# Inverse edge counts of a relational graph layer: narrow one-hots, four array columns, a result kept relation by destination

## The chip, the cores and the metric

The kernel runs on one core of a Trainium2 chip. The core's engines work side by side and meet through semaphores: TensorE (PE) multiplies matrices into PSUM, its weight loads are listed as PEld; VectorE (DVE) and ScalarE (ACT) do elementwise work; GpSimd (POOL) issues the gathers by index; SyncE (SP) issues most other transfers. The metric is the device time of one execution in microseconds, lower is better; times of several executions are given as their median.

## The reference, cut to what matters

A graph of 3125 nodes with 128 features has 103,125 directed edges, sorted by destination, each with a type from 0 to 15. A four-layer graph convolution is followed by three relational layers. One relational layer is:

```python
seg = tgt * R + edge_type                      # R = 16 relations
msg = x[src]
agg = segment_sum(msg, seg, N * R).reshape(N, R, d)
cnt = segment_sum(ones, seg, N * R).reshape(N, R, 1)
agg = agg / clip(cnt, 1.0)
out = einsum('nrd,rdo->no', agg, W_r) + x @ root_r + bias_r
```

The counts depend on the edges alone and are the same in all three layers. So they are made once, and every layer multiplies its sums by 1/max(count, 1).

## The kernel before, in words

The kernel first packs and indexes the edges, then runs the convolution's first three layers (adjacency blocks built from one-hots, multiplied at L811), then the fourth aggregation, then the relational layers. The program is written as interleaved generators and handed to a scheduler that fixes each engine's order when the program is built; at run time every engine works through its list in order.

**The fourth aggregation** (L1195 to L1217, about 1007 to 1158 us of the profile). Seven column groups of up to four node blocks. For each block of 128 nodes, 25 matmuls (L1207, 384 columns) accumulate in a PSUM tile p_a of a four-buffer pool; VectorE evacuates it in three steps (L1212). `first_rows` normalizes finished blocks, transposes them (L1189) and stores them as rows of the table from which the first relational layer gathers.

**The counts** are made in the same time by the generator `relation_tiles`, of which a step is run before most node blocks. The destinations are taken in 49 groups of 64. A group's edges fill at most 18 tiles of 128 edges, so there are 882 tiles, laid out as c (7 sets of groups), k (18 tiles), g (7 groups in a set). A packed word per edge is gathered (L728); `relative` makes the destination within the group, `to_edges` turns it so that edges lie on partitions (transposes at L748, copies at L754). In the same way go the type, the combined key `16 * destination + type`, from which the start of the tile's window is taken off first, and the source index. Since edges are sorted, tile k of a group can only reach the destinations `WIN[k]` of its 64: between 5 and 17 of them.

To count, `hot` (L796) makes two one-hots for 21 tiles at a time: hr, 64 wide, of the destination, and ht, 16 wide, of the type. Each tile is one matmul (L1161): hr as weights (64 columns), ht moving (16 columns), added into PSUM at partitions 0 or 64 by the group's parity. All of it fits one bank, pc: 128 partitions by 400. A maximum with 1 and a reciprocal (L1169 to L1171) give wi, and one transfer writes it to winv_d as rows of destinations with the 16 relations inside (L1172).

**The relational layers** (1165 us to the end) run `rgcn_mixed`. For each of 25 node blocks, `loads` fetches the slots sr and two tiles wv, each 64 destinations' inverse counts broadcast to all partitions (L1346). Even groups are computed from X in place: one-hots G and S (L1421, L1425), matmuls L1445 (four array columns of 32) and L1488 into p_p, a pool of one buffer, with a rest at L1494. Odd groups are computed from gathered messages (L1369): one-hots sel (L1455), matmuls L1469 into p_a, two buffers. Both accumulators hold 32 destinations by 16 relations, relation innermost. `scaled` (L1363) multiplies such an accumulator by its half of wv and writes gs relation by destination, 1024 bytes from one relation to the next. `project` then takes gs relation by relation into the weights (L1379), and `rows_out` stores the new rows. The multiply is done 294 times: 150 from p_p, 144 from p_a. After each p_p multiply the next L1488 starts a new sum in the same buffer.

A second branch, `rgcn_gathered`, holds the same multiply; it is built but not taken with these inputs.

Of the kernel before, what the change touches and what calls it, by code (L numbers as in the profile page):

```python
# [10 lines left out]
F32 = mybir.dt.float32  # L11
F16 = mybir.dt.float16
# [3 lines left out]
ALU = mybir.AluOpType  # L16
# [5 lines left out]
P = 128  # L22
N = 3125
NB = 25
NP = NB * P
NR = 16
# [600 lines left out]
def regular(ctx: ExitStack, tc: tile.TileContext, a: dict, out: bass.AP, c_d, s_d, h_d, dinv):  # L627
# [45 lines left out]
    with ExitStack() as gx:  # L673
# [10 lines left out]
        adj_d = [dram.tile([P, NB * 4 * P], BF, name=f"adj_d{q}") for q in range(NQ)]  # L684
        winv_d = dram.tile([NP, NR], F32, name="winv_d")

# [105 lines left out]

        def hot(pool, numbers, table, width, t0, n, name, room=None):

            o = pool.tile([P, room or n, width], F16, name=name)[:, :n, :]
            nc.vector.tensor_tensor(  # L796
                o.rearrange("p t (c w) -> p t c w", w=2),
                numbers[:, :width].rearrange("p (c w) -> p c w", w=2)[:, None, :, :].to_broadcast([P, n, width // 2, 2]),
                table[:, t0:t0 + n, None, :].to_broadcast([P, n, width // 2, 2]), op=ALU.is_equal)
            return o  # L800
# [321 lines left out]
        def relation_tiles():  # L1122

            with tc.tile_pool(name="tr", bufs=1) as tw, tc.tile_pool(name="trh", bufs=2) as th:
                w, at = gathered_words(tw, RR, TR, 7, CR, GR)
                yield
                rel, d_i = relative(tw, w, at)
                rel2 = tw.tile([P, CR * RR, 2], F16, name="rel2")
                to_edges(tw, rel, RR, CR, dup(rel2, 1))
                typ2 = tw.tile([P, CR * RR, 2], F16, name="typ2")  # L1130
                typ = tw.tile([RR, CR, P], F32, name="typ")
                nc.vector.tensor_scalar(d_i, w, 12, NR - 1, op0=ALU.logical_shift_right, op1=ALU.bitwise_and)
                nc.vector.tensor_copy(typ, d_i)
                to_edges(tw, typ, RR, CR, dup(typ2, 0))
                yield
                nc.vector.scalar_tensor_tensor(rel, rel, float(NR), typ, op0=ALU.mult, op1=ALU.add)
                lo_f = tw.tile([RR, 1], F32, name="lo_f")
                nc.vector.memset(lo_f, 0.0)
                p_f = tw.tile([RR, 1], F32, name="pr_f")
                iota(nc, p_f, [[0, 1]], 1)  # L1140
                more = tw.tile([RR, 1], F32, name="more")
                for k in range(1, TR):
                    nc.vector.tensor_scalar(more, p_f, 7.0 * k, float(NR * (WIN[k][0] - WIN[k - 1][0])),
                                            op0=ALU.is_ge, op1=ALU.mult)
                    nc.vector.tensor_add(lo_f, lo_f, more)
                nc.vector.tensor_scalar(rel, rel, lo_f, None, op0=ALU.subtract)
                to_edges(tw, rel, RR, CR, dup(key2, 1))
                nc.vector.tensor_scalar(d_i, w, 4095, None, op0=ALU.bitwise_and)
                nc.vector.tensor_copy(typ, d_i)
                to_edges(tw, typ, RR, CR, lambda t0, m, p: nc.vector.tensor_copy(src_t[:, t0:t0 + m], p))  # L1150
                yield
                pc = ps_b.tile([P, 512], F32, name="p_b")
                for c in range(CR):
                    for k0 in range(0, TR, 3):
                        t0 = c * RR + k0 * 7
                        hr = hot(th, iota_k, rel2, GR, t0, 21, "hr")
                        ht = hot(th, iota_k, typ2, NR, t0, 21, "ht")
                        for t in range(21):
                            g = c * 7 + t % 7
                            o = 64 * (g % 2)  # L1160
                            nc.tensor.matmul(pc[o:o + 64, (g // 2) * NR:(g // 2 + 1) * NR], hr[:, t, :], ht[:, t, :],  # L1161
                                             start=(c == 0 and k0 == 0 and t < 2),
                                             stop=(c == CR - 1 and k0 == TR - 3 and t >= 19), skip_group_check=True)
                    yield
                wi = tw.tile([P, NB, NR], F32, name="wi")
                nc.vector.memset(wi, 1.0)
                full = (NB - 1) * NR
                wf = wi.rearrange("p b r -> p (b r)")
                nc.vector.tensor_scalar_max(wf[:, :full], pc[:, :full], 1.0)  # L1169
                nc.vector.tensor_scalar_max(wf[:64, full:], pc[:64, full:NB * NR], 1.0)  # L1170
                nc.vector.reciprocal(wf, wf)  # L1171
                nc.sync.dma_start(winv_d.rearrange("(b p) r -> p b r", p=P), wi)  # L1172
                yield
# [50 lines left out]
    def rgcn_gathered(xT):  # L1224
        with ExitStack() as rx:
# [44 lines left out]
            for l in range(3):  # L1270
# [7 lines left out]
                for b0 in range(0, NB, 2):  # L1278
# [3 lines left out]
                    for g in groups:  # L1282
                        wv = wvp.tile([P, GR * NR], F32, name="wv")
                        nc.sync.dma_start(wv, winv_d[g * GR:(g + 1) * GR, :].rearrange("n r -> (n r)")[None, :]
                                          .to_broadcast([P, GR * NR]))
                        for h, p in enumerate(gathered(g, tabs[l % 2])):
                            n0 = (g - 2 * b0) * GR + 32 * h
                            nc.vector.tensor_tensor(gs[:, :, n0:n0 + 32].rearrange("p r n -> p n r"),
                                                    p.rearrange("p (n r) -> p n r", r=NR),
                                                    wv[:, h * 512:(h + 1) * 512].rearrange("p (n r) -> p n r", r=NR),  # L1290
                                                    op=ALU.mult)
# [24 lines left out]
    def rgcn_mixed(X):  # L1316

        with ExitStack() as rx:
# [20 lines left out]
            def loads(b):  # L1339
# [4 lines left out]
                for g in range(2 * b, min(2 * b + 2, NGR)):  # L1344
                    t = wvp.tile([P, GR * NR], F32, name="wv")
                    nc.sync.dma_start(t, winv_d[g * GR:(g + 1) * GR, :].rearrange("n r -> (n r)")[None, :]  # L1346
                                      .to_broadcast([P, GR * NR]))
                    wv.append(t)
                return sr, wv

            def layer(l, X, Xn):
# [9 lines left out]

                def scaled(gs, p, wv, n0):
                    nc.vector.tensor_tensor(gs[:, :, n0:n0 + 32].rearrange("p r n -> p n r"),  # L1363
                                            p.rearrange("p (n r) -> p n r", r=NR),
                                            wv.rearrange("p (n r) -> p n r", r=NR), op=ALU.mult)

# [41 lines left out]
                for at, b in enumerate(order):  # L1408
# [10 lines left out]
                    for q in range(4):  # L1419
# [18 lines left out]
                        for half in range(2):  # L1438
# [12 lines left out]
                            for _ in range(plan[2 * q + half] if two else 0):  # L1451
# [23 lines left out]
                                if k == TR:  # L1475
                                    for h in range(2):
                                        scaled(gs, pa[h], wv[1][:, h * 512:(h + 1) * 512], b % 2 * P + GR + 32 * h)
                            if todo:
# [4 lines left out]
                            def spread(pb=pb, m=m, S=S, q=q, half=half, b=b, gs=gs, wv=wv, Sx=Sx if q % 2 else None,  # L1483
# [8 lines left out]
                                if q % 2 and half:  # L1492
                                    for i in range(3):
                                        nc.tensor.matmul(pb, mx[:, i, :], Sx, start=False, stop=(i == 2),  # L1494
                                                         skip_group_check=True)
                                    scaled(gs, pb, wv[0][:, q // 2 * 512:(q // 2 + 1) * 512], b % 2 * P + 32 * (q // 2))
                                    if q == 3 and (b % 2 or b == NB - 1):
# [43 lines left out]
```

## Time and profile before

| | us |
|---|---|
| median of 3 runs | 3061.7 (3061.36 to 3063.99) |
| profiled execution, its time | 3064.4 |
| its span in the profile | 3062.5 |
| PE / DVE / POOL / ACT busy | 2700.7 / 1800.2 / 1456.5 / 1088.2 |
| one-hots hr and ht (L796) | 42 x 850 ns and 42 x 319 ns |
| count matmuls (L1161) | 882 |
| maxima and reciprocal (L1169, L1170, L1171) | 0.56, 0.16 and 2.63 |
| multiply by inverse counts (L1363) | 294 x 1044 ns |

The span is that of one execution under the profiler, so sums are made against it and then carried to the median. A busy share says how long an engine worked, not whether anything waited for it; the chain of work that ended last follows, step by step back from the end, what released what. A matmul's end is modelled, so its start-to-start distance is the better measure of its cost.

### The profile page before, as it was taken

What the parts mean: (1) busy time and instruction counts of PE and PEld (TensorE: products, weight loads), DVE (VectorE), ACT (ScalarE), POOL (GpSimd) and SP (SyncE); (2) the same over time, 40 slices, a digit from 0 to 9 for tenths busy, and PEclk for the clock granted to TensorE, in tenths of its full rate; (3) what the DMA queues carried; (4) which work ended last, traced back from release to release, by engine and by line L of the source; (5) the groups of instructions that cost most, each with busy time, mean ns of one, the idle gap of its engine ahead of it and who ended that gap; (6) DMA issues with size and microseconds to landing.
All of it is one profiled execution on the core that took longest, in us unless ns stands there. A gap on an engine that the chain in (4) does not pass through costs nothing.

```text
span 3062.5 us, 62721 instructions
## 1 busy us (share of the span) xinstructions
PE 2700.7 (88%) x25427; PEld 1797.7 (59%) x25427; DVE 1800.2 (59%) x3710; ACT 1088.2 (36%) x2657; POOL 1456.5 (48%) x1472
## 2 busy tenths in 40 slices
PE   0377679999999897999999999999999999999998
PEld 0244345545555564777666666666666666667666
DVE  6886886757663784555555445454555455545453
ACT  0333433222222213444444344343444443434343
POOL 4100000000000005777777757777777577777775
PEclk9988879999999997999999999999999999999999
DMA  5111113222211535555555545555555455555553
GB/s 162 33 70 60 44 44 141 87 88 99 88 60 44 191 129 156 163 153 153 162 151 149 153 138 157 147 155 146 162 145 152 124 155 151 151 149 151 150 151 90
DMA packets 179105, 386.78 MB, mean 126 GB/s; under 512 B 49831, under 2 KB 128902, under 8 KB 175732
## 3 DMA queue, kind: packets, MB, share of 16 engines
q1 hardware_dynamic: 100708, 232.22, 23.3%
q0 software_dynamic: 68480, 141.38, 16.8%
q10 hardware_dynamic: 9616, 9.08, 1.0%
q8 instruction: 201, 3.29, 0.4%
q14 instruction: 100, 0.82, 0.1%
HBM read 350.25 MB, written 32.30 MB: 125 GB/s over the span
## 4 chain that ended last, share of the span: by engine, by line
PE 69%; DVE 15%; DMA 11%; issue 3%; POOL 1%; ACT 1%; another core or an unknown queue 0%; DVEq 0%; POOLq 0%; SPq 0%; ACTq 0%
PE p_p L1488 18%; PE p_a L811 15%; DMA msg<-tab,src_t 9%; PE p_m L1379 9%; PE p_g L1445 8%; PE p_a L1469 8%; DVE gs L1363 3%; PE p_a L1207 3%; DVE ov L796 2%; DVE ou L796 2%; PE p_m L825 2%; PE p_b L874 2%; PE p_p L1494 1%; DMA seg<-f_d,at_i 1%; POOL msg L1369 1%
## 5 line engine op out<-in xcount | busy, mean ns | idle before, releaser
L1369 POOL DMA_INDIRECT msg<-tab,src_t x1296 | 1325.6, 1023 | 400.1 <-issue 110.6
L1447 ACT CAST m<-p_g 128x384 bf16<-128x384 f32 x1800 | 748.9, 487 | 738.8 <-PE p_g L1445 737.6
L1488 PE MATMUL p_p<-S,m 128*128 128x256 bf16 x5400 | 697.6, 274 | 21.0 <-DVE gs L1363 16.0
L1425 DVE TENSOR_TENSOR S<-iota_k,key_s 128x1536 bf16<-128x1536 f16 x300 | 287.5, 959 | 629.2 <-PE p_p L1488 628.8
L1488 PEld LDWEIGHTS <-m 128*128 128x128 bf16 x5400 | 488.8, 98 | 260.3 <-issue 206.6
L1469 PE MATMUL p_a<-sel,msg 128*128 128x144 bf16 (+9 forms) x4536 | 437.9, 239 | 91.0 <-DMA msg<-tab,src_t 89.9
L1469 PEld LDWEIGHTS <-msg 128*128 128x128 bf16 x4536 | 342.5, 98 | 165.8 <-DMA msg<-tab,src_t 100.1
L1455 DVE TENSOR_TENSOR sel<-iota_k,key 128x1248 bf16<-128x1248 f16 (+2 forms) x216 | 198.7, 920 | 133.1 <-PE p_a L1469 133.0
L1445 PE MATMUL p_g<-X,G 128*32 128x384 bf16 x4800 | 273.2, 331 | 0.2
L1379 PE MATMUL p_m<-gs,Wr 128*128 128x256 f32 (+1 forms) x1248 | 267.1, 372 | 1.7 <-DVE gs L1363 1.7
L874 PE MATMUL p_b<-ov,ou 128*128 128x200 f16 x1200 | 169.9, 293 | 111.0 <-DVE ou L796 88.9
L1379 PEld LDWEIGHTS p_m<-gs,Wr 128*128 128x128 f32 x1248 | 230.5, 191 | 32.9 <-DVE gs L1363 2.8
L1445 PEld LDWEIGHTS <-G 128*32 128x32 bf16 x7200 | 138.0, 95 | 143.3 <-issue 88.7
L874 PEld LDWEIGHTS <-ou 128*128 128x128 f16 x1200 | 119.9, 113 | 161.0 <-DVE ou L796 125.9
L811 PE MATMUL p_a<-adj,x3b 128*128 128x512 bf16 (+1 forms) x1050 | 212.8, 356 | 0.0
L1421 DVE TENSOR_TENSOR G<-sr,pid 128x768 bf16<-128x768 f16 x300 | 166.4, 555 | 77.1 <-PE p_g L1445 70.9
L811 PE MATMUL p_a<-adj,x3a 128*128 128x512 bf16 (+1 forms) x1050 | 211.1, 356 | 0.0
L413 POOL IOTA pp<- 128x1 f32 x1 | 0.1, 138 | 414.6 <-PE p_b L874 414.6
L1363 DVE TENSOR_TENSOR gs<-p_a,wv 128x512 f32<-128x512 f32 x144 | 150.4, 1044 | 38.6 <-PE p_a L1469 34.2
L1363 DVE TENSOR_TENSOR gs<-p_p,wv 128x512 f32<-128x512 f32 x150 | 156.6, 1044 | 8.2 <-PE p_p L1494 8.2
L811 PEld LDWEIGHTS <-x3a 128*128 128x128 bf16 x1050 | 95.3, 98 | 97.4
L811 PEld LDWEIGHTS <-x3b 128*128 128x128 bf16 x1050 | 95.7, 98 | 95.4
(343 smaller groups left out, 2505.1 us busy)
## 6 DMA issues: line engine op xcount, KB each, us to landing
wv<-winv_d SPq DMA_DIRECT2D x147, 512.0 KB
adj<-adj_d SPq DMA_DIRECT2D x18, 3200.0 KB
sr<-slots_d SPq DMA_DIRECT2D x75, 768.0 KB
msg<-tab,src_t POOLq DMA_INDIRECT x1296
adj_d<-adj SPq DMA_DIRECT2D x6, 3200.0 KB
tab<-X SPq DMA_DIRECT2D x50, 96.0 KB
adj<-adj_d SPq DMA_DIRECT2D x3, 800.0 KB
tab<-Xn SPq DMA_DIRECT2D x25, 96.0 KB
```

The lines of the kernel that those rows point to most:

```text
L811: nc.tensor.matmul(p[k][:, :n], x3_[:, i, s, k * P:(k + 1) * P], adj[:, i, :n], start=(i == 0 and s == 0), stop=(i == NB - 1 and s == 2))
L874: nc.tensor.matmul(pb[:, gg * IA:(gg + 1) * IA], hot_u[k][:, g + gg, :], hot_v[k][:, g + gg, :], start=(gg == 0 and k == 0), stop=(gg == 1 ...
L1363: nc.vector.tensor_tensor(gs[:, :, n0:n0 + 32].rearrange("p r n -> p n r"), p.rearrange("p (n r) -> p n r", r=NR), wv.rearrange("p (n r) - ...
L1369: nc.gpsimd.indirect_dma_start(out=m.rearrange("p s d -> p (s d)"), out_offset=None, in_=table, in_offset=bass.IndirectOffsetOnAxis(ap=at, ...
L1379: nc.tensor.matmul(po[:, :n], W[:, r, :], gs[:, r, :n], start=False, stop=(r == NR - 1))
L1421: nc.vector.tensor_tensor(G.rearrange("p (c w) -> p c w", w=2), sr[:, q, :].rearrange("p (c w) -> p c w", w=2), pid[:, None, :].to_broadca ...
L1425: nc.vector.tensor_tensor(S.rearrange("p j (c w) -> p j c w", w=2), iota_k[:, :GS * NR].rearrange("p (c w) -> p c w", w=2)[:, None, :, :] ...
L1445: nc.tensor.matmul(pg[o:o + 32, :3 * D], G[:, i * 32:(i + 1) * 32], X[:, i, :, :].rearrange("p s d -> p (s d)"), start=True, stop=True)
L1447: nc.scalar.copy(m[:, t, :], pg[:, :3 * D])
L1455: nc.vector.tensor_tensor(s6[:, :, :n6].rearrange("p j (c w) -> p j c w", w=2), iota_k[:, :n6].rearrange("p (c w) -> p c w", w=2)[:, None, ...
L1469: nc.tensor.matmul(pa[h][:, (a0 - 32 * h) * NR:(a1 - 32 * h) * NR], msgs[k][:, i, :], s6[:, k % 6, (a0 - lo) * NR:(a1 - lo) * NR], start=( ...
L1488: nc.tensor.matmul(pb[:, o:o + GS * NR], m[:, t, i * D:(i + 1) * D], S[:, 3 * half + t, :], start=(q % 2 == 0 and half == 0 and t == 0 and ...
```

## The change

The counts are made the other way round, narrower, and kept the other way round:

- The window's start is taken off the destination before it is turned (and the result is cut at 100), so rel2 holds numbers within the window, 0 to 16. The key is made from rel2 and typ2 where the edges already lie on partitions; its own turning, seven transposes and two copies, goes.
- One-hots are made for 42 tiles (six k) at a time. hr is only as wide as the widest window among them: 14, 16 or 18 in rows of 18. ht stays 16 wide.
- The matmul has ht as weights (16 columns) and hr's window moving (6 to 18 columns). Its result is 16 relations on partitions, destinations along the row. Group g goes to partitions 32 * (g % 4), columns of bank g // 32: two banks, four array columns. `ends` marks the first and last matmul of each bank and column.
- Maxima and reciprocal are done in two batches, after set 4 and after the last set, over 16 of every 32 partitions. wi is set to 1 by POOL.
- winv_d is kept as group, relation, destination, written by four transfers, one for each array column.
- The multiply reads wv by relation inside destination, at a distance of 64 words from one relation to the next.

```diff
-        winv_d = dram.tile([NP, NR], F32, name="winv_d")
+        winv_d = dram.tile([NGR, NR, GR], F32, name="winv_d")
...
-        def hot(pool, numbers, table, width, t0, n, name, room=None):
-
-            o = pool.tile([P, room or n, width], F16, name=name)[:, :n, :]
+        def hot(pool, numbers, table, width, t0, n, name, room=None, wide=None):
+
+            o = pool.tile([P, room or n, wide or width], F16, name=name)[:, :n, :width]
...
                 rel, d_i = relative(tw, w, at)
+                lo_f = tw.tile([RR, 1], F32, name="lo_f")
+                nc.vector.memset(lo_f, 0.0)
+                p_f = tw.tile([RR, 1], F32, name="pr_f")
+                iota(nc, p_f, [[0, 1]], 1)
+                more = tw.tile([RR, 1], F32, name="more")
+                for k in range(1, TR):
+                    nc.vector.tensor_scalar(more, p_f, 7.0 * k, float(WIN[k][0] - WIN[k - 1][0]),
+                                            op0=ALU.is_ge, op1=ALU.mult)
+                    nc.vector.tensor_add(lo_f, lo_f, more)
+                nc.vector.tensor_scalar(rel, rel, lo_f, 100.0, op0=ALU.subtract, op1=ALU.min)
...
-                nc.vector.scalar_tensor_tensor(rel, rel, float(NR), typ, op0=ALU.mult, op1=ALU.add)
-                lo_f = tw.tile([RR, 1], F32, name="lo_f")
...
-                nc.vector.tensor_scalar(rel, rel, lo_f, None, op0=ALU.subtract)
-                to_edges(tw, rel, RR, CR, dup(key2, 1))
+                nc.vector.scalar_tensor_tensor(key2, rel2, float(NR), typ2, op0=ALU.mult, op1=ALU.add)
...
-                pc = ps_b.tile([P, 512], F32, name="p_b")
+                pc = [ps_b.tile([P, 512], F32, name="p_b") for _ in range(2)]
+                wi = tw.tile([P, 13, GR], F32, name="wi")
+                nc.gpsimd.memset(wi, 1.0)
+                wf = wi.rearrange("p g n -> p (g n)")
+                seen = {}
                 for c in range(CR):
-                    for k0 in range(0, TR, 3):
+                    for k in range(TR):
+                        for g in range(7 * c, 7 * c + 7):
+                            seen.setdefault((g // 32, g % 4), []).append((c, k, g))
+                ends = {v[i]: i for v in seen.values() for i in (0, -1)}
+                for c in range(CR):
+                    for k0 in range(0, TR, 6):
                         t0 = c * RR + k0 * 7
-                        hr = hot(th, iota_k, rel2, GR, t0, 21, "hr")
-                        ht = hot(th, iota_k, typ2, NR, t0, 21, "ht")
-                        for t in range(21):
-                            g = c * 7 + t % 7
-                            o = 64 * (g % 2)
-                            nc.tensor.matmul(pc[o:o + 64, (g // 2) * NR:(g // 2 + 1) * NR], hr[:, t, :], ht[:, t, :],
-                                             start=(c == 0 and k0 == 0 and t < 2),
-                                             stop=(c == CR - 1 and k0 == TR - 3 and t >= 19), skip_group_check=True)
+                        wd = (max(WIN[k][1] - WIN[k][0] for k in range(k0, k0 + 6)) + 2) // 2 * 2
+                        hr = hot(th, iota_k, rel2, wd, t0, 42, "hr", wide=18)
+                        ht = hot(th, iota_k, typ2, NR, t0, 42, "ht")
+                        for t in range(42):
+                            k, g = k0 + t // 7, c * 7 + t % 7
+                            lo, hi = WIN[k]
+                            o, n0 = 32 * (g % 4), g // 4 % 8 * GR
+                            nc.tensor.matmul(pc[g // 32][o:o + NR, n0 + lo:n0 + hi + 1], ht[:, t, :],
+                                             hr[:, t, :hi + 1 - lo], start=ends.get((c, k, g)) == 0,
+                                             stop=ends.get((c, k, g)) == -1, skip_group_check=True)
+                    if c in (4, CR - 1):
+                        h, c0, c1 = (0, 0, 512) if c == 4 else (1, 512, 13 * GR)
+                        for i in range(4):
+                            m = c1 - c0 if h == 0 or i == 0 else c1 - c0 - GR
+                            nc.vector.tensor_scalar_max(wf[32 * i:32 * i + NR, c0:c0 + m],
+                                                        pc[h][32 * i:32 * i + NR, :m], 1.0)
+                        nc.vector.reciprocal(wf[:, c0:c1], wf[:, c0:c1])
                     yield
-                wi = tw.tile([P, NB, NR], F32, name="wi")
-                nc.vector.memset(wi, 1.0)
-                full = (NB - 1) * NR
-                wf = wi.rearrange("p b r -> p (b r)")
-                nc.vector.tensor_scalar_max(wf[:, :full], pc[:, :full], 1.0)
-                nc.vector.tensor_scalar_max(wf[:64, full:], pc[:64, full:NB * NR], 1.0)
-                nc.vector.reciprocal(wf, wf)
-                nc.sync.dma_start(winv_d.rearrange("(b p) r -> p b r", p=P), wi)
+                for i in range(4):
+                    n = len(range(i, NGR, 4))
+                    nc.sync.dma_start(winv_d[i:NGR:4, :, :].rearrange("g r n -> r g n"), wi[32 * i:32 * i + NR, :n, :])
...
-                    nc.sync.dma_start(t, winv_d[g * GR:(g + 1) * GR, :].rearrange("n r -> (n r)")[None, :]
+                    nc.sync.dma_start(t, winv_d[g].rearrange("r n -> (r n)")[None, :]
...
-                def scaled(gs, p, wv, n0):
+                def scaled(gs, p, wv, n1, n0):
                     nc.vector.tensor_tensor(gs[:, :, n0:n0 + 32].rearrange("p r n -> p n r"),
                                             p.rearrange("p (n r) -> p n r", r=NR),
-                                            wv.rearrange("p (n r) -> p n r", r=NR), op=ALU.mult)
+                                            wv.rearrange("p (r n) -> p n r", r=NR)[:, n1:n1 + 32, :], op=ALU.mult)
```

## The prediction

> **What bounds the kernel now.** I read the page's totals first, then the chain of work that ended last, then two stretches closely: the fourth aggregation, where the counts are made, and the relational stage, where they are used. The table of stretches (us from the span's start; after each engine's time the instructions that touch the stretch):
>
> ```profile
> core 0: us, PE busy (x) PEld busy (x) DVE busy (x) ACT busy (x) POOL busy (x), PEclk, DMA share, GB/s
> ...
> 1056.90:1121.20 64.30, 64.17 (x1131) 39.89 (x1131) 60.87 (x173) 6.64 (x26) 0.00 (x0) 1.00 0.38 143
> 1121.20:1165.00 43.80, 37.21 (x226) 21.78 (x224) 30.73 (x116) 11.29 (x44) 0.13 (x1) 0.98 0.32 91
> ...
> 1210.00:3062.00 1852.00, 1744.18 (x18727) 1245.98 (x18726) 956.28 (x1364) 769.00 (x1909) 1370.08 (x1339) 0.99 0.52 148
> ```
>
> The counts fill the first of these; TensorE has no gap there and VectorE is 95% busy. The third is the relational stage, 1852 of 3062.5 us, with TensorE at 94% and VectorE at 52%. Inside the count stretch TensorE's timeline alternates:
>
> ```profile
> 1062.99 0.55 PE L1161 MATMUL p_b<-ht,hr 128*64 128x16 f16 x21
> 1063.47 0.82 PE L1207 MATMUL p_a<-x3a,adj 128*128 128x384 bf16 x4
> 1064.22 0.55 PE L1161 MATMUL p_b<-ht,hr 128*64 128x16 f16 x21
> ```
>
> A period is 1.23 us: four aggregation matmuls, and 21 count matmuls from 1062.99 to 1063.47. Aggregation matmuls alone follow each other every 0.1625 us (60 in 9.75 us at 1130), so four are 0.65. The block of counts costs 0.58: the first block of 42 ran at 20.4 ns each, so 21 are 0.43, and 0.15 goes on changing over and back.
>
> In the relational stage VectorE multiplies each finished accumulator by the inverse counts (L1363). Groups by shape, then the chain in order of time at one such place, then the waits:
>
> ```profile
> L1363 DVE TENSOR_TENSOR gs<-p_p,wv 128x512 f32<-128x512 f32 x150 | 156.6, 1044 | 8.2 <-PE p_p L1494 8.2
> L1363 DVE TENSOR_TENSOR gs<-p_a,wv 128x512 f32<-128x512 f32 x144 | 150.4, 1044 | 38.6 <-PE p_a L1469 34.2 <-PE p_m L1379 4.0
> ...
> L1057 DVE TENSOR_TENSOR F<-t,fe 128x125 f16<-128x125 f16 x4 | 2.7, 677 | 0.0
> ...
> L1042 DVE TENSOR_TENSOR fe<-fe,tm 128x125 f32<-128x125 f32 x4 | 1.2, 290 | 0.1
> ```
> ```profile
> 1504.10 0.19 issue
> 1504.29 1.06 DVE gs L1363
> 1505.35 0.04 issue
> 1505.39 1.14 PE p_p L1488 x9
> ```
> ```profile
> PE p_p L1488 <- DVE gs L1363: 16.0, 64, 0.4
> ```
>
> The waits make L1363 look harmless: 16 us. The chain does not. The pool behind p_p holds one buffer, so the next group's first L1488 matmul cannot start until the multiply has read it. Over the trace's records, 117 of 149 such multiplies have an L1488 matmul starting 52 to 53 ns after their end. TensorE happened to be busy until shortly before, so the wait looks short; there is no slack. From 1210 to the end the chain gives L1363 5.6%, that is 104 us or 99 multiplies. So each nanosecond on L1363 costs 99 to 117 ns of time; I take 105 times. The p_a multiplies have slack, because that pool has two buffers and nothing restarts on their end.
>
> [...]L1363 writes gs in steps of 256 words. L738 fixes the base, 896 elements in 1092 ns and 1664 in 1889, so 1.04 ns each plus 162. Then (1044-162)/512 = 1.72 ns. L1057, with 2-byte data and both a source and the result strided by small steps, costs 3.1 ns per element over L1042 of the same width.[...]
>
> **The change, part by part.**
>
> *The multiply reads across.* wv now holds 16 rows of 64, and L1363 walks it by relation inside destination: each element hops 64 words where it came in runs of 16. Destination and PSUM operand stay. No row of this trace shows a source hop beside a destination hop. Lower bound: it hides under the write hop, 0. Upper bound: the same penalty again, (1.72-1.04)x512 = 348 ns[...].[...] I take 110[...]. 105 x 0.110 = **+11.6 us**[...]. The order of instructions in the relational stage is the same on every engine, and wv's loads carry the same bytes, still 4 KB in a run.
>
> *Count matmuls.* 882 before and after, now with 16 columns of weights and 6 to 18 moving columns in four column groups. In the built program they stand in 15 stretches between other TensorE work, where the trace has 41: 26 x 0.152 = **-4.0 us**. [...]I take 18, 882 x 2.4 ns = **-2.1 us**, bounds 0 and -9.
>
> *One-hots.* Before, 42 x 850 + 42 x 319 ns = 49 us of VectorE. By the slope between the 336- and 1536-wide rows (0.533 ns each plus 140), widths 588, 672 and 756 cost 453, 498 and 543, seven of each, and 21 of 672 cost 498: 21 us. The 28 us are worth nothing by themselves: TensorE had no gap to close. They pay for what follows.
>
> *Inverse counts.* Before 3.7 us (memset, two maxima, reciprocal at 2.63). After: maxima 4 x 0.69 + 0.49 + 3 x 0.43, reciprocals by 6.6 ns a column 3.4 + 2.1: 10 us of VectorE. The first batch stands between two count blocks: 2.8 + 0.5 + 3.4 us before the next one-hot. TensorE has some 6.5 us of other work queued there. With pairs of blocks that meet a just-finished one-hot, **+1.5 us** (0 to 3). The memset goes to POOL, idle from 1007.4 until the word gather at 1019.7; a late one would cost its microsecond. The inverse counts leave in four transfers of 256-byte runs, not one: three more SP issues at 0.38 us near 1125, ahead of the last rows' stores, and first read after 1165. Nothing, with 40 us of cover.
>
> *Front.* The subtraction of window starts (0.68 us) now precedes the first transposes, on which TensorE waits 5.70 us. Its 34 small operations stay in the gather's shadow at 1009 to 1019. The third set of transposes is that of the sources, and the keys come from one VectorE operation on 1764 elements: [...]ahead of the evacuations that TensorE waits for at 1042.69. Queued behind it also stand two one-hots more. Together the restart is 0.4 to 2.5 us later; from it goes the 1.1 us of source transposes later on, and two casts (2.1 us of VectorE, hidden). **+1.3 us**, net.
>
> Sum: 11.6 - 4.0 - 2.1 + 1.5 + 1.3 = +8.3 us. On the profiled execution, span 3062.5 and time 3064.4, that is 3070.8 and 3072.7; on the median of the runs, 2.7 us lower, **3070**.
>
> **The rivals.**
> - *A, partial adding (0.52).* As summed: [...]7 to 15 us against 3 saved; 3064 to 3077.
> - *B, the read hop hides (0.23).* If the source's penalty overlaps the write's, the relational stage is unchanged and the count stage decides: -3, or -10 if the count matmuls fall to 10 ns, +3 if evacuations and keys hold TensorE up. 3052 to 3065, centre 3058. The point is a multiply below 1044 + 30 ns. For it: [...]a stretch where TensorE is full.[...]
> - *C, the penalties add (0.25).* The multiply takes 1.39 us or more, 105 x 0.35 = +37, less 3: 3096[...]. For it: L1057 shows 3 ns extra with strides on both sides. Against: those steps are small, of 2-byte data.
>
> **How the numbers follow.** 0.2% is 6 us, about what can be told from no change. B gives a third of its chance to faster (0.09), the rest to same (0.14); A's low end, a quarter of it, adds 0.13 to same; the rest of A and all of C are slower: 0.64. The range leaves out B's low end and C's upper half: 3056 to 3100.[...]
>
> **What would show it.** L1377, the multiply's new line, at 1.10 to 1.19 us, its chain share from 1210 on rising from 5.6% to above 6%, and that stage longer by about 105 times the difference. A multiply at 1.05 means B, above 1.35 C. Count matmuls (L1173) at 18 ns and 15 stretches; the aggregation's last matmul 3 us earlier than 1158. The prediction falls if the multiplies with 53 ns to the next L1488 gain slack, or if L1173 runs slower than 20.4 ns.

## The result, and the profile after

| | before | after |
|---|---|---|
| median of 4 runs each, us | 3062.84 (3061.36 to 3065.45) | 3095.34 (3092.64 to 3097.15) |
| ratio, 95% interval | | 1.0104 [1.0087, 1.0122] |
| span of the profiled execution | 3062.5 | 3093.9 |
| first gather of the relational stage starts at | 1166.1 | 1161.6 |
| from there to the end | 1896.5 | 1932.2 |

The change makes the kernel 1% slower. The front and the counts gain 4.4 us; the relational stage, whose instructions stand in the same order on every engine, loses 35.8. The table of stretches after (us from the start; then each engine's busy time) answers to the one of before:

```profile
core 0: us, PE busy (x) PEld busy (x) DVE busy (x) ACT busy (x) POOL busy (x), PEclk, DMA share, GB/s
...
1056.90:1121.20 64.30, 58.61 (x1179) 35.51 (x1179) 54.74 (x179) 9.98 (x40) 0.13 (x1) 1.00 0.42 159
1121.20:1165.00 43.80, 32.74 (x198) 19.19 (x195) 25.62 (x89) 8.84 (x35) 2.75 (x3) 0.90 0.37 101
1210.00:3093.00 1883.00, 1752.27 (x18663) 1244.32 (x18661) 985.84 (x1362) 767.26 (x1905) 1401.96 (x1335) 0.99 0.51 145
```

In the count stretch TensorE was busy for 64.17 of 64.30 us; it now has 5.7 us of gaps. In the relational stage (last line, 31 us longer than its counterpart) TensorE gained 8 us of busy time, VectorE 30 and POOL 32. The front and the counts on TensorE's timeline:

```profile
1035.54 1.71 PE L748 MATMUL p_b<-ident,rel 126*128 126x126 f32 x7 [7.50 <-DVE rel L1138]
...
1045.04 9.12 PE L1221 MATMUL p_a<-x3a,adj 128*128 128x384 bf16 x40 [2.35 <-DVE x_sb L1226]
...
1060.68 0.82 PE L1173 MATMUL p_b<-hr,ht 128*16 128x6 f16 x84
```

From the first of 84 count matmuls to the aggregation matmul after them it takes 0.76 us, 9.0 ns each; counted in this way, the first 42 of the old form took 20.4 each. From start to start inside a block without gaps it is 7.0 to 7.8 ns, where it was 18.1 to 18.5. In the trace the moving side has 5 to 17 columns, not 6 to 18. The first line waits 7.50 us, 1.8 more than before, and the aggregation restarts at 1045.04, 2.35 later.

The multiply, and the gathers, from the page's groups after (then mean ns of one, then idle time just before it):

```profile
L1383 POOL DMA_INDIRECT msg<-tab,src_t x1296 | 1357.2, 1047 | 398.6 <-PE p_a L1483 113.2
...
L1377 DVE TENSOR_TENSOR gs<-p_a,wv 128x512 f32<-128x512 f32 x144 | 158.1, 1098 | 38.5 <-PE p_a L1483 34.0
L1377 DVE TENSOR_TENSOR gs<-p_p,wv 128x512 f32<-128x512 f32 x150 | 163.5, 1090 | 9.4 <-PE p_p L1508 9.4
```

and the gathers' group before, which the prediction did not show:

```profile
L1369 POOL DMA_INDIRECT msg<-tab,src_t x1296 | 1325.6, 1023 | 400.1 <-issue 110.6 <-PE p_a L1469 110.0 <-PE p_p L1488 65.5
```

The multiply takes only 50 ns more. The gathers, which the change does not touch, take 24 ns more each, 31.6 us in all, about what the kernel lost (32.5). The idle time before them is the same, 400.1 and 398.6 us, or 0.31 us each, whatever it is put down to. The waits and the chain after, at a place like the one shown of before:

```profile
PE p_a L1483 <- DMA msg<-tab,src_t: 107.1, 86, 13.8
...
PE p_p L1502 <- DVE gs L1377: 19.6, 69, 0.4
```
```profile
1337.63 0.19 issue
1337.82 1.11 DVE gs L1377
1338.94 0.04 issue
1338.98 1.14 PE p_p L1502 x9
```

TensorE's wait for gathered messages was 89.9 us in 69 waits; it is now 107.1 in 86. The chain still runs through the multiply, and 114 of 149 (117 before) still have an L1502 matmul 53 ns after their end. But the multiply's share of the chain fell from 5.6% to 5.2%, where the prediction wanted it above 6%.

### The profile page after: what moved, and what is told of

The parts are those of the page before. It is cut to its first block, busy times and chain, and to the rows that moved or that the text cites. A ratio compares the mean times of both kernels' runs of the same rounds, so it can differ in the third digit from the quotient of the medians.

```text
span 3093.9 us, 62653 instructions
## 1 busy us (share of the span) xinstructions
PE 2699.3 (87%) x25420; PEld 1789.7 (58%) x25420; DVE 1815.0 (59%) x3672; ACT 1087.7 (35%) x2657; POOL 1492.0 (48%) x1473
## 4 chain that ended last, share of the span: by engine, by line
PE 66%; DVE 16%; DMA 12%; issue 3%; ACT 1%; POOL 1%; another core or an unknown queue 0%; DVEq 0%; POOLq 0%; ACTq 0%; SPq 0%
PE p_p L1502 18%; PE p_a L811 15%; DMA msg<-tab,src_t 10%; PE p_g L1459 9%; PE p_m L1393 8%; PE p_a L1483 8%; DVE gs L1377 3%; DVE ov L796 2%; DVE ou L796 2%; PE p_a L1221 2%; PE p_m L825 2%; PE p_b L874 2%; PE p_p L1508 1%; DMA seg<-f_d,at_i 1%; DVE S L1439 1%
## 5 line engine op out<-in xcount | busy, mean ns | idle before, releaser
L1383 POOL DMA_INDIRECT msg<-tab,src_t x1296 | 1357.2, 1047 | 398.6 <-PE p_a L1483 113.2
L1502 PE MATMUL p_p<-S,m 128*128 128x256 bf16 x5400 | 700.3, 275 | 25.8 <-DVE gs L1377 19.6
L1502 PEld LDWEIGHTS <-m 128*128 128x128 bf16 x5400 | 489.6, 98 | 266.5 <-issue 209.8
L1483 PE MATMUL p_a<-sel,msg 128*128 128x144 bf16 (+9 forms) x4536 | 443.4, 240 | 108.5 <-DMA msg<-tab,src_t 107.1
L1377 DVE TENSOR_TENSOR gs<-p_a,wv 128x512 f32<-128x512 f32 x144 | 158.1, 1098 | 38.5 <-PE p_a L1483 34.0
L1377 DVE TENSOR_TENSOR gs<-p_p,wv 128x512 f32<-128x512 f32 x150 | 163.5, 1090 | 9.4 <-PE p_p L1508 9.4
L946 POOL DMA_INDIRECT w<-c_d,at x4 | 4.8, 1206 | 306.2 <-DMA slots_d<-ro 294.7
```

The source lines that it names most:

```text
L1383: nc.gpsimd.indirect_dma_start(out=m.rearrange("p s d -> p (s d)"), out_offset=None, in_=table, in_offset=bass.IndirectOffsetOnAxis(ap=at, ...
L1483: nc.tensor.matmul(pa[h][:, (a0 - 32 * h) * NR:(a1 - 32 * h) * NR], msgs[k][:, i, :], s6[:, k % 6, (a0 - lo) * NR:(a1 - lo) * NR], start=( ...
L1502: nc.tensor.matmul(pb[:, o:o + GS * NR], m[:, t, i * D:(i + 1) * D], S[:, 3 * half + t, :], start=(q % 2 == 0 and half == 0 and t == 0 and ...
```

## What the gathers say

GpSimd issues 1371 gathers from 1161.6 on. Summed over the trace of each kernel (us), the relational stage from the first gather to the end is:

| | before | after |
|---|---|---|
| the gathers' own durations | 1404.3 | 1439.0 |
| gaps under 0.4 us between gathers, some 304 ns each | 416.2 (1366 gaps) | 416.5 (1367) |
| longer gaps (the two between layers hold 46 and 49) | 52.8 (4) | 53.0 (3) |
| after the last gather | 23.2 | 23.7 |
| the stage | 1896.5 | 1932.2 |

GpSimd is never idle for longer than some 0.30 us between gathers except at four places. Its queue of gathers is full from end to end, and it bounds the stage, though the page shows it busy for 74% and TensorE for 94%. So what lengthens gathers lengthens the kernel, microsecond for microsecond: +34.7 and +35.8.

And what lengthens them? A gather during which VectorE does nothing, or only multiplies, takes 942 to 963 ns in both traces (median 946 to 947). Of the 392 gathers over 980 ns of before (after 1200 us), 391 started while a one-hot (S, Sx, G or sel) ran on VectorE and end 808 to 830 ns after that one-hot's end. After the change 465 of 466 started under a one-hot; 433 end 813 to 828 ns after its end, and 32 as long after the end of the next one, which followed at once.

Who starts first decides. The gathers that started before a one-hot, by as little as 10 ns, were never lengthened: 446 before and 371 after, all of 941 to 963 ns. Of those that started under a one-hot with over 160 ns left of it, 391 of 397 were lengthened before and 463 of 468 after, and the 11 others had started within 33 ns of it. Of those that started under the multiply in the same way (147 before, 136 after), none was lengthened, so the hop in the multiply does not slow a gather directly.

The one-hots compare two operands in SBUF; the multiply, under which none of 147 and 136 gathers was lengthened, reads one from SBUF and one from PSUM. In these two traces the two kinds differ in that, among other things. The number of operands in SBUF does not settle it: run a_gts below has a one-hot that reads one tensor from SBUF and still holds gathers (71 of 94). By what means a one-hot holds a gather, no run shows; measured is the end, some 820 ns after the one-hot's, where an undisturbed gather takes 945 in all.

The same place in both traces, VectorE and then POOL, each time first before and then after:

```profile
1339.76 1.05 DVE L1363 TENSOR_TENSOR gs<-p_a,wv 128x512 f32<-128x512 f32 x1
1340.65 0.54 DVE L1421 TENSOR_TENSOR G<-sr,pid 128x768 bf16<-128x768 f16 x1
1341.11 0.99 DVE L1455 TENSOR_TENSOR sel<-iota_k,key 128x1632 bf16<-128x1632 f16 x1
```
```profile
1339.30 1.37 POOL L1369 DMA_INDIRECT msg<-tab,src_t  x1 [0.30 <-PE p_a L1469]
1340.97 1.04 POOL L1369 DMA_INDIRECT msg<-tab,src_t  x1 [0.30 <-issue]
1342.31 0.95 POOL L1369 DMA_INDIRECT msg<-tab,src_t  x1 [0.30 <-issue]
```
```profile
1334.15 1.11 DVE L1377 TENSOR_TENSOR gs<-p_a,wv 128x512 f32<-128x512 f32 x1
1335.18 0.54 DVE L1435 TENSOR_TENSOR G<-sr,pid 128x768 bf16<-128x768 f16 x1
1335.65 0.99 DVE L1469 TENSOR_TENSOR sel<-iota_k,key 128x1632 bf16<-128x1632 f16 x1
```
```profile
1333.72 1.33 POOL L1383 DMA_INDIRECT msg<-tab,src_t  x1 [0.30 <-PE p_a L1483]
1335.36 2.10 POOL L1383 DMA_INDIRECT msg<-tab,src_t  x1 [0.30 <-issue]
1337.77 0.96 POOL L1383 DMA_INDIRECT msg<-tab,src_t  x1 [0.30 <-PE p_a L1483]
```

The second gather of each is the same one. Before, it started 0.32 us after G and ended at 1342.01, 0.82 after G's end. After, G starts 1.03 us after the multiply in place of 0.89, the gather meets it 0.18 us after its start, and ends at 1337.46, 0.82 after the end of sel: it lost G and then all of sel. Gathers over 1.9 us: none before, 23 after. Over all gathers after 1200 us, the time above 945 ns is 105.9 us before and 140.6 after; the part tied to the end of sel grew from 12.9 to 39.5, that of Sx from 0.1 to 6.7, that of G from 25.4 to 28.9, and that of S fell from 66.2 to 64.2.

Note the 0.89 and 1.03. Where another instruction follows at once, the multiply's start to the next start went from 896 to 997 ns for p_p and from 891 to 1006 for p_a (medians): 101 and 115 ns more, or some 1.95 ns per word. Its result comes only 50 ns later, because the overlap with the next instruction shrank from 155 to 98 ns. The mean duration hides half of what the change costs VectorE.

## The experiments

Chips of two kinds served. On the first kind, as in the comparison above, before takes about 3064 us; on the second it takes about 3634, nearly all of the difference in the relational stage, so each ratio below is against before on the same chip. The first four runs fell on a chip of the second kind. The theories then: T1, the multiply's length is amplified in the loop of multiply, TensorE and gathers; R1, the hopping access itself disturbs; R2, the new layout and earlier start do it. The expectations of the first runs call T1 theory 1 and R2 theory 2.

**b_hop: the hop alone, in the kernel before.**

```diff
-                                            wv.rearrange("p (n r) -> p n r", r=NR), op=ALU.mult)
+                                            wv.rearrange("p (r n) -> p n r", r=NR)[:, n1:n1 + 32, :], op=ALU.mult)
```

> The kernel before, with the multiply reading the inverse counts across (64 words from one element to the next, so they are the wrong counts); nothing else differs, also no engine's order. Theory 1, the hop lengthens the multiply by some 50 ns and the relational stage makes more of it than 105 times that: multiply 1.09 us, time 3098 (+35, of which 5 direct). Theory 2, the hop adds only its 50 ns on the path and the rest of the loss lies in the new layout or in the earlier start of the relational stage: 3068.

Measured: 3645.20 us, ratio 1.0043 [1.0028, 1.0058], some +15.5 us by the ratio, with the multiply at 1080 and 1092 ns.

**a_runs: the change without the hop** (the reverse of that edit, in the changed kernel).

> The changed kernel, with the multiply reading the inverse counts in runs of 16 as before (so the wrong ones); count stage and layout stay new. Theory 1: the relational stage is back to its old length, and the count stage's gain of about 6 us is all that is left: 3057. Theory 2: only the direct 5 us go: 3090.

Measured: 3625.38 us, 0.9984 [0.9971, 0.9997], multiply 1035 and 1041 ns. With b_hop this puts a loss on the multiply's read and leaves the count stage a small gain. The change itself was not run on this chip, so R2 stood until b_hop_2.

**b_split: the multiply in two halves, in the kernel before.**

```diff
-                    nc.vector.tensor_tensor(gs[:, :, n0:n0 + 32].rearrange("p r n -> p n r"),
+                    for h in range(2):
+                        o = 256 * h
+                        nc.vector.tensor_tensor(gs[:, :, n0 + 16 * h:n0 + 16 * h + 16].rearrange("p r n -> p n r"),
...
```

> The kernel before, the multiply cut in two of 256 elements each, reading in runs; result unchanged. No hop, but each pair takes longer by one fixed cost[...]. If any lengthening is multiplied (theory 1 in its plain form), 3062 plus five times 294 x 0.1, so +60 to +120. If the loss belongs to the hop[...], only the direct cost shows: 105 x 0.1, +8 to +17, 3070 to 3079.

Measured: 3625.81 us, 0.9984 [0.9964, 1.0003]. It looks like the fall of T1 and is not, since the two halves together take no longer than the whole: see b_split_2.

**a_rel: the even groups' accumulator also relation by destination.** The keys of the even groups are renumbered, so that their multiply reads and writes adjacent words in all operands.

```diff
-                        nc.vector.scalar_tensor_tensor(fr[:, 4, :], rel, float(NR), t, op0=ALU.mult, op1=ALU.add)
+                        nc.vector.scalar_tensor_tensor(fr[:, 4, :], t, float(GS), rel, op0=ALU.mult, op1=ALU.add)
...
+                def scaled_rel(gs, p, wv, n1, n0):
+                    nc.vector.tensor_tensor(gs[:, :, n0:n0 + 32].rearrange("p r (q n) -> p q r n", q=2),
+                                            p.rearrange("p (q r n) -> p q r n", q=2, r=NR),
...
```

> The changed kernel with the keys of S and Sx ordered type x 16 + destination, so that p_p also is relation by destination and its multiply runs over 16 adjacent words in all three operands; the p_a multiply still hops. p_p's multiply 0.70 us instead of 1.09. Theory 1 and the prediction's step that p_p's multiply is on the path: at least 105 x 0.39 = 41 us less than the changed kernel, 3054, and down to 3030 if more is made of it. If the p_p multiplies have slack, under 10 us less: 3087.

Measured: 3621.86 us, 0.9968 [0.9954, 0.9982], the even groups' multiply at 685 ns.

The second four fell on a chip of the first kind.

**after_2: the change again.**

> The changed kernel once more, beside the kernel before on the chip that this batch gets. On the chip of the first comparison it took 32 us more than before; on the chip of the first four experiments before itself takes 570 us more, and the parts of the change tried there add up to about +8 us (hop +15.5, count stage -8). If the extra time of the change is a property of the program (every theory so far), this run shows +32 us on a chip where before takes about 3063 us, and about +8 us (ratio 1.002) on one where it takes about 3634 us.

Measured: 3094.41 us, 1.0087 [1.0067, 1.0106].

**b_hop_2.**

> The kernel before with nothing changed but the order in which the multiply reads its inverse counts (hopping 64 words; the values it meets are then those of other destinations, so its numbers are not the reference's). On a chip where before takes about 3063 us: T1 and R1, by which the multiply's form alone does the harm in the relational stage, give +30 to +40 us; R2, by which the new layout of the count stage and the earlier start of the gathers do it, gives +6 us (115 path multiples of 50 ns) or less. On one where before takes about 3634 us: +15 us again.

Measured: 3105.34 us, 1.0122 [1.0103, 1.0142], +41 us between the medians and +37 by the ratio. The hop alone does all of the harm, and R2 falls: the stage lasts 1941.3 us here and 1941.1 in after_2, whose first gather starts 5.1 us earlier thanks to its count stage. The groups of this run show the changed kernel's gathers, without its counts:

```profile
L1369 POOL DMA_INDIRECT msg<-tab,src_t x1296 | 1371.6, 1058 | 398.7 <-PE p_a L1469 112.0 <-issue 100.8 <-PE p_g L1445 66.7
```

**b_split_2.**

> The kernel before with each multiply cut in two halves, same values, each pair some 150 ns longer than the whole. T1, by which it is the length of the multiply that is amplified in the loop of multiply, TensorE and gathers (36 us for 50 ns): +60 to +120 us on a chip where before takes about 3063 us. R1, by which the hop and not the length does the harm: 115 path multiples of 150 ns, +17 us, or less where the first half's result is early. On one where before takes about 3634 us: within 10 us of before.

Measured: 3063.65 us, 0.9997 [0.9988, 1.0007]. Its groups:

```profile
L1371 POOL DMA_INDIRECT msg<-tab,src_t x1296 | 1328.9, 1025 | 396.7 <-issue 112.1 <-PE p_a L1471 106.7 <-PE p_p L1490 62.8
...
L1365 DVE TENSOR_TENSOR gs<-p_p,wv 128x256 f32<-128x256 f32 x300 | 156.4, 602 | 8.9 <-PE p_p L1496 8.9
```

Two halves of 602 ns are not 1204: the second starts 440 ns after the first, and the pair lasts 1043 on average, as the whole did (1044). Nothing was made longer, so nothing was tested; the gathers (1025 ns) and the time stayed.

**a_rel_2.**

> The changed kernel with the keys of the even groups renumbered (destination*16+type becomes type*16+destination within a tile of 16), so that their multiply goes over adjacent words in all three operands: 685 ns in place of 1090 on the other chip, the odd groups' multiply stays at 1090. If the even groups' multiply is what sets the relational stage's time: 115 path multiples of -400 ns off the changed kernel's +32, about -14 us against before on a chip where before takes about 3063 us. If the odd groups' hop is what disturbs, the time stays above before, at +10 to +30 us.

Measured: 3041.75 us, 0.9922 [0.9903, 0.9942]: faster than both kernels, by 22.6 us than before and 53 than the change. Its groups:

```profile
L1389 POOL DMA_INDIRECT msg<-tab,src_t x1296 | 1303.2, 1006 | 398.7 <-issue 113.1 <-PE p_a L1489 101.3 <-PE p_p L1508 68.2
...
L1382 DVE TENSOR_TENSOR gs<-p_p,wv 128x512 f32<-128x512 f32 x150 | 102.5, 683 | 8.6 <-PE p_p L1514 8.6
```

Only 3 of 150 even multiplies now have a matmul bound to their end, so TensorE's path through the multiply is gone. By time alone the path theory comes near here, with -14 us expected of it and -22.6 measured; what tells it apart is that the stage again follows the gathers: their sum is 1381.3 us, 23.0 less than before, and the stage 1874.6, 21.9 less.

The next three fell on a chip of the second kind again. They were to part the even groups' multiply from the odd ones', and length from access.

**b_hop_pp and b_hop_pa: the hop in one kind of multiply** (in the kernel before, `scaled` kept for the other).

> The kernel before with the hopping read in the even groups' multiply (p_p) alone; its inverse counts are then those of other destinations. Hopping in both multiplies cost 41 us. The path theory (the even groups' multiply is what TensorE waits for, the odd groups' has slack): all of it, +30 to +45 us. If the odd groups' multiply matters as much (it delays the release of message buffers and the next one-hots on VectorE): about half, +15 to +25 us.

> The kernel before with the hopping read in the odd groups' multiply (p_a) alone. The path theory, and the step of the prediction that gave these multiplies slack: within 5 us of before. If what counts is VectorE's time as a whole, which shifts the one-hots against the gathers: +15 to +25 us.

Measured: 3642.97 us, 1.0021 [1.0008, 1.0034], for the even groups; 3641.58, 1.0024 [1.0010, 1.0038], for the odd ones. By the ratios that is +7.6 and +8.7 us, each about half of b_hop's +15.5: on this kind of chip the odd groups' multiplies have no slack either.

**b_long: longer without a hop.**

```diff
+                    nc.vector.tensor_tensor(gs[:, :, n0 + 30:n0 + 32].rearrange("p r n -> p n r"),
+                                            p[:, 480:].rearrange("p (n r) -> p n r", r=NR),
+                                            wv[:, 480:].rearrange("p (n r) -> p n r", r=NR), op=ALU.mult)
```

> The kernel before, no hop, values unchanged: after each multiply its last 2 destinations (32 words) are multiplied once more, which ends the pair some 50 ns later (32 of 512 words at 1.7 ns each), about what the hop adds. If the length of the multiply does the harm: +30 to +45 us, like the hop. If the hopping access itself does[...]: +6 us, the direct path of 115 multiples of 50 ns, or less.

Measured: 3651.96 us, 1.0052 [1.0033, 1.0070], +19 us by the ratio, where the hop cost 15.5. Its groups:

```profile
L1372 POOL DMA_INDIRECT msg<-tab,src_t x1296 | 1342.0, 1035 | 801.0 <-PE p_a L1472 351.8 <-issue 209.2 <-PE p_g L1448 145.5
...
L1491 PE MATMUL p_p<-S,m 128*128 128x256 bf16 x5400 | 789.7, 297 | 192.7 <-DVE gs L1366 139.6 <-issue 16.8 <-DVE Sx L1437 14.1
...
L1366 DVE TENSOR_TENSOR gs<-p_p,wv 128x32 f32<-128x32 f32 x150 | 30.2, 201 | 0.1
```

This run did not test what it was made for. In the built order the short instruction does not follow the multiply: in 141 of 150 even groups an Sx one-hot stands between. Sx starts 882 ns after the multiply, the short instruction 1206, and it ends at 1407, some 370 ns after the multiply's own end and not 50. It also reads p_p, so TensorE now waits for it, 139.6 us in all. What the run shows is a later release and another order of VectorE's instructions; length and access are not parted. Besides, GpSimd idles 801 us before these gathers, 0.62 each: on this kind of chip its queue is not full, and the runs made there speak of another bound. Their sizes do not carry over. Whether a longer multiply without a hop costs as much as the hop was shown on neither kind.

**a_gts: a shorter one-hot G, in the changed kernel.**

```diff
-                        nc.vector.tensor_tensor(G.rearrange("p (c w) -> p c w", w=2),
...
+                        nc.vector.tensor_scalar(G, sr[:, q, :], pid, None, op0=ALU.is_equal)
```

> The changed kernel, its multiply and inverse counts as they are, with the one-hot G of the even groups made by a comparison against one number per partition (one input from memory in place of two[...]; values unchanged). The lock theory: a gather that is issued while a 16-bit one-hot (two inputs in SBUF) runs on VectorE does its last 820 ns only after that one-hot's end; 466 of 1,343 gathers of the changed kernel are lengthened so, by 154 us in all (106 us before the change), and this, not the multiply's 50 ns as such, makes the +31 us. Then a shorter G takes away part of it, though no multiply changes: gathers tied to the end of G lose two thirds of their 28 us, the gathers' mean falls below 1,035 ns, and the time falls by 15 to 35 us from the changed kernel's, to about 3,070 us or less on a chip where before takes about 3,063 us (on one where it takes about 3,634 us, by 5 to 15 us from the changed kernel's +8 there). The path theory without locks: TensorE's waits for VectorE end with the multiply, G has slack, the time stays within 5 us of the changed kernel's.

Measured, on a chip of the first kind: 3112.57 us, 1.0157 [1.0138, 1.0176], some 15 us slower than the change. Its groups:

```profile
L1383 POOL DMA_INDIRECT msg<-tab,src_t x1296 | 1378.5, 1064 | 397.7 <-PE p_a L1481 109.1 <-issue 100.9 <-PE p_g L1457 68.0
...
L1435 DVE TENSOR_SCALAR G<-sr,pid 128x768 bf16<-128x768 f16 x300 | 127.3, 425 | 70.2 <-PE p_g L1457 65.0 <-DMA sr<-slots_d 5.1
```

G fell from 556 to 425 ns, but with one tensor and one number per partition it still holds gathers. Of the 94 that started under it with over 160 ns left, 71 were lengthened: 26 until 0.82 us after G's own end, and 45 until 0.82 after the end of the sel that follows, each over 1.9 us. The other 23 had started within 93 ns of G. The gathers tied to G's end did fall, from 119 with 27.7 us (after_2) to 26 with 2.2: fewer started under it (94 for 141), more of these got in first (23 for 3), and more were held through sel (45 for 30). But those tied to sel rose from 47.6 to 57.9 us and those tied to S from 69.5 to 86.9. The hold was shortened and not removed. The expectation of a gain was wrong by its sign; both theories put down for this run missed the time.

What holds through all of them is the sum over GpSimd. Profiled executions on chips of the first kind (us; "above 945" counts gathers after 1200 us):

| | gathers' sum | above 945 ns | stage | stage minus gathers | span |
|---|---|---|---|---|---|
| a_rel_2 | 1381.3 | 83.3 | 1874.6 | 493.3 | 3035.7 |
| before | 1404.3 | 105.9 | 1896.5 | 492.2 | 3062.5 |
| b_split_2 | 1407.6 | 109.5 | 1898.2 | 490.6 | 3069.0 |
| after | 1439.0 | 140.6 | 1932.2 | 493.2 | 3093.9 |
| after_2 | 1452.1 | 153.8 | 1941.1 | 489.0 | 3103.6 |
| b_hop_2 | 1453.0 | 155.0 | 1941.3 | 488.3 | 3109.1 |
| a_gts | 1458.2 | 159.8 | 1947.5 | 489.3 | 3109.3 |

The gathers vary by 77 us, the rest of the stage by 5. Two executions of the changed kernel, after and after_2, differ by 13 us in their gathers, so a smaller difference between two rows says little.

**What stays open.** That the hop alone makes the loss, that the gathers' sum is the stage's time on the first kind of chip, and that their excess is tied to one-hots under which they start, is shown. That with some 100 ns more on the multiply more of them start under one-hots (468 for 397, with over 160 ns left) and wait through sel is seen in the traces. Why the new order of meetings is a worse one, and whether the multiply's length, its hopping access or its later result brings it about, no run settles. Nor is it settled why a gather that meets G ends after G in one case and after sel in another: after the change, gathers that started 189 to 317 ns after G got in before sel, and others that started 170 to 428 ns after it did not. No run took the one-hots away from the gathers with all else left alone.

## Why the prediction was right or wrong

The direction was right, and 3095 lies within 3056 to 3100. But the forecast of 3070 was 25 us short, a loss of 8 us where 32.5 was measured, and the range reached so far only because of rival C, whose mechanism did not occur. That 3095 lies inside is luck. Step by step:

- **What bounds the relational stage: wrong, and the root of the miss.** TensorE at 94% and a chain through the multiply were taken for the bound. GpSimd's line, 1370 us in 1339 instructions, was in the table shown and not read: with 0.30 us between gathers it is full on this chip. The step that failed is "each nanosecond on L1363 costs 99 to 117 ns of time". It held for the first 25 even multiplies, which drift by 50 ns each against before (from -6.2 to -5.1 us); then irregular steps in the waits for gathers take over, to +31 at the end.
- **The multiply, +110 ns: right as VectorE's time, half as latency.** 101 and 115 ns from start to next start, 50 at the result; L1377 took 1.09 and 1.10 us, where 1.10 to 1.19 was the mark. The 110 was the author's estimate between bounds of 0 and 348; no row of the trace before shows it. Measured from start to next start it is 997 and 1006 ns for 512 words, some 1.95 each, where before it was 896 and 891, some 1.75. By the prediction's own path the 50 ns would cost 105 x 0.05 = 5 us, not 11.6; the stage lost 35.8, and the mechanism, not the size, was off.
- **"The p_a multiplies have slack": wrong on the second kind of chip,** where they cost as much as the p_p ones (b_hop_pa). On the first kind no run tried them alone.
- **"The order of instructions is the same", so nothing else moves: wrong.** The order is the same and the phase is not.
- **Count matmuls: 15 stretches as said; the rate was mis-sized.** 9.0 ns, not 18: 882 x (20.4 - 9.0) = 10 us, for which -2.1 was taken, just beyond its bound of -9; the 18 and the bound were the author's estimates. It was not all kept, since TensorE now waits for VectorE: 5.7 us of gaps in the stretch.
- **One-hots and inverse counts: near.** ht took 497 and hr 455 to 545 ns; the reciprocals 3.35 and 2.15 us. TensorE waits 3.9 us for ht, where +1.5 was taken for the first batch.
- **Front: upper half.** The restart is 2.35 us later (0.4 to 2.5 said), the first transposes 1.8; the key operation took 2.00 us for 1764 elements, the rate of L738 before (1.04 ns each plus 162 is 1997).
- **Count stage in sum: near, with parts whose errors offset each other.** -4.0 - 2.1 + 1.5 + 1.3 = -3.3 said; the first gather is 4.4 us earlier, the aggregation's last matmul 4.6.
- **A sum that does not come out.** A's 7 to 15 us less 3 give 3065 to 3073, not 3064 to 3077. It does not bear on the miss.
- **Rivals.** A had the multiply's cost and not its consequence. B needed a multiply under 1074 ns; it took 1090. C needed 1.39 us.
- **The marks set beforehand.** The prediction was to fall if the tied multiplies gained slack; they did not, 114 of 149. The mark that did speak was the chain share, which fell, and the stage's length against 105 times the difference: 5 us by that rule, 36 measured.

## What to carry to other kernels

Before calling the busiest engine the bound, look at the gaps of the others. Here GpSimd had the same gap of some 0.30 us between gathers at all but four places of the stage, and the stage followed its gathers (+34.7 and +35.8 us), though it was busy for 74% and TensorE for 94%. Where gathers fill a stage as they do here, look at what VectorE runs when a gather starts: in this kernel 391 of 397 gathers that started under a one-hot with over 160 ns left were lengthened, and an edit that touches no gather took their mean from 1023 to 1047 ns. And take a VectorE instruction from start to next start, not by its duration: the multiply's duration grew by 50 ns, its distance to the next instruction by 101 and 115.

## What the runs showed of the hardware

- Consecutive VectorE instructions overlapped: the one after a 128x512 multiply of 1044 ns started 891 to 896 ns after the multiply's start (before), and two halves of 602 ns started 440 apart and took 1043 together (b_split_2), so cutting the multiply in two cost nothing (3063.65 us, 0.9997).
- A 128x512 multiply from PSUM took 683 ns with adjacent words in all operands (a_rel_2), 1044 when the result hops 256 words (before), 1090 to 1098 when one input hops 64 words as well (after).
- An indirect gather with VectorE idle or multiplying took 942 to 963 ns, median 946 to 947 (before, after). Of those that started while a one-hot ran with over 160 ns left, 391 of 397 (before) and 463 of 468 (after) were lengthened. Of all gathers over 980 ns, 391 of 392 (before) and 433 of 466 (after) ended 808 to 830 ns after the end of that one-hot, and 32 (after) as long after the end of the next. Those that started before a one-hot took 941 to 963 (446 and 371 gathers), and of those that started under a multiply with one input in PSUM (147 and 136) none was lengthened.
- Count matmuls with 16 weight columns in four column groups started every 7.0 to 7.8 ns (after), those with 64 in two groups every 18.1 to 18.5 (before).
- Chips of two kinds ran all stages up to the first gather alike, to about 2 us, and the relational stage in 1875 to 1948 and in 2456 to 2488 us. On the second kind GpSimd idled 0.62 us before a gather (b_long) where it is 0.31 on the first (before, after); the mean granted clock of the profiled executions was 0.903 to 0.912 where it was 0.961 to 0.970, and from 1300 us on 0.90 (b_hop) where it was 0.99 (before). Much of TensorE's idle time there is put down to issue (333 us of its weight loads at L1448 alone in b_long); the cause was not looked for further.
